# A graph layer on one core: single instead of double turns, gates per unit, and lists read after the stores of h

## The chip, the core and the metric

The kernel runs on one core of one Trainium2 chip. A core has five engines with a queue of their own each: TensorE (PE in the profile; its weight loads are shown apart as PEld), VectorE (DVE), ScalarE (ACT), GpSimd (POOL) and SyncE (SP, which here only issues transfers). Transfers are issued by SP, ScalarE or GpSimd and are done by 16 DMA engines. An engine works through its queue in order; an instruction that waits holds up all that is queued behind it. The metric is the device time of one launch in microseconds (us).

## The reference

The input is a graph with 6250 nodes of 256 features and 206250 edges that are sorted by target node, each with a polarity and 64 features. Cut to what matters:

```
h = max(layernorm(x), 0)                                  # every node
e = relu(raw @ W_e1.T + b_e1) @ W_e2.T + b_e2             # every edge, 64 -> 256 -> 256
edge_emb = (e * (clip(attr[:, 0], 0, 1) + 0.01)) @ W_le.T + b_le
msg  = relu(h[src] + edge_emb)                            # one row of h is gathered per edge
aggr = segment_sum(msg, dst)                              # 6250 rows
y = (h + aggr) @ W_g1.T + b_g1
out = x + relu(layernorm(y) * ln_g + ln_b) @ W_g2.T + b_g2
```

## The kernel before, in words

**Tiles.** Edges are taken in tiles of 128. Four tiles are a *block* (512 edges), two tiles a *unit* (256 edges), so a block has two units; two blocks are a *pair* (four units). There are 403 blocks, NU = 806 units and NP = 202 pairs. Six blocks are a *group*; the sums of a group are built up in PSUM.

**Start phase.** x is loaded in 13 parts of up to four times 128 rows. For each part VectorE takes the statistics, ScalarE applies layernorm and ReLU, GpSimd adds b_le (`hb`, four adds of 128x256 for a whole part, L470) and SP stores the part to `hb_d` in device memory. W_e2 and W_le are multiplied into one matrix `wc_s` in this phase. The edge parts of the first LEAD = 22 units are made here too. ScalarE's queue issues the reads of three lists of 806 KB: the source nodes `src_s`, the target nodes `dst_f` and the polarities `pol_s`; GpSimd casts `dst_f` to float at the end. The first four units gather rows of x itself, by a small list `src_0` of 8 columns. All other units gather rows of h from `hb_d`, so the first of these gathers stands behind the last store of h and behind the list `src_s`.

**What is done for a unit.** TensorE makes the edge part, 2 x 2 matmuls with `wc_s` into one PSUM bank (L347; a float32 matmul stands in the profile as two records, so a unit has 8). VectorE adds an offset and moves it to SBUF as `msg` (L353). GpSimd issues two gathers for the unit, one for each tile (L663), into one of HG = 20 places `hx`/`hg`. When a gather has landed, VectorE multiplies `msg` by the polarity and adds it to the gathered rows (the unit's two *products*, L718), and ScalarE applies ReLU to both halves (L725). Later TensorE sums the rows by target node with a 0/1 matrix `sel` (L740).

**What is done for a pair.** The first layer of the edge network, raw @ W_e1 (L310), runs for a whole pair, two pairs ahead: two halves of 128 features for each of two blocks, 4 matmuls (8 records) into 4 banks, two of them side by side in the two halves of the array's rows. ScalarE evicts three of the banks and VectorE one. The bias, ReLU and eviction are one instruction. Raw edge features for two pairs come in one transfer of 512 KB.

**PSUM.** Edge parts, first layers and node work take their banks from one ring of BANKS = 7. A matmul into a bank waits for the reader that emptied it seven takes earlier.

**The order of the work** is written out by the program. `forward(u)` emits the edge part of unit u, and behind unit u with u % 4 == TURN = 1 the *turn* (`turn_of`): first layers, sums and loads of raw. In the middle of the run (pairs FEW = 6 to NP - FEW - 1 = 195, `by_two`) a turn is done for two pairs at once, behind every eighth unit: sums of two pairs, then first layers of two pairs. Before and behind that it is done for each pair: first layer, then sums. A unit's products are due a number of units behind its edge part (`lag`), 18 at first and one less every SHRINK = 44 units, so TensorE starts 22 units ahead of the gathers and ends one unit ahead of them. Node work (layernorm, two 256x256 matmuls and two transposes for each of 49 windows of 128 nodes: L174, L189, L207, L220) is put between units in pieces, except directly around a turn (QUIET).

**When gathers are issued** is set by a planner. `in_step` (called as `paced`) adds up the planned TensorE time in `spent`: EDGE = 1.754 for a unit, LAYER = 0.9 for half a first layer, SUMS = 0.46 for the sums of a block, NODES = 0.81 for a node piece. A gather is planned at STEP = 1.288 each. At a *gate* (two places in a double turn's round: behind unit u % 8 == 5, and at the first layers) it emits all gathers up to `spent + AFLOAT + HALF`, where AFLOAT = 6.0 and HALF is half a round, 10.5; the first of them waits for the TensorE instruction at hand, the others for nothing but their places and lists.

**Lists and row numbers.** `first_rows` on TensorE reads `dst_f` (L566), and `rows_of_edges` on VectorE makes the row numbers from which `sel` is built.

Of the kernel before, what the change touches and what calls it, by code (L numbers as in the profile page):

```python
# [9 lines left out]
F32 = mybir.dt.float32  # L10
# [7 lines left out]
P = 128  # L18
N = 6250
D = 256  # L20
# [25 lines left out]
HALF = 4 * EDGE + 2 * LAYER + 2 * SUMS + NODES  # L46
BANKS = 7
SHRINK = 44
RAW = 4
HG = 16 + RAW  # L50
# [51 lines left out]
def gnn_kernel(ctx: ExitStack, tc: tile.TileContext, x, src_c, dst_c, dst_r, pol_c, raw_t, w_e1t, w_e2,  # L102
# [141 lines left out]
    with fast:  # L244
# [5 lines left out]
        msg_p = big.enter_context(tc.tile_pool(name="msg", bufs=LEAD + 2))  # L250
# [6 lines left out]
        evictions = {}  # L257
        places = [hx_p.tile([P, 2, D], F32, name=f"hx{i}") for i in range(RAW)]
        users = {}

# [23 lines left out]
        def load_pair(q):  # L284
            if q >= NP:
                return
# [9 lines left out]
        def first_layer(q):  # L296
# [7 lines left out]
            for c in range(2):  # L304
# [15 lines left out]
                paced(LAYER, z[c], c == 0 and not (by_two(q - 2) and q % 2))  # L320
# [17 lines left out]
        def edge_part(u):  # L338
# [10 lines left out]
            msg[u] = msg_p.tile([P, 2, D], F32, name="msg")  # L349
# [12 lines left out]
        paced = lambda us, behind, gate=False: None  # L362
# [40 lines left out]
        src_0 = const.tile([P, 2 * RAW], I32, name="src_0")  # L403
# [3 lines left out]
        nc.scalar.dma_start(out=src_0, in_=src_c[:, :2 * RAW])  # L407
# [25 lines left out]
        with tc.tile_pool(name="p1", bufs=4) as p1, tc.tile_pool(name="p1x", bufs=11) as p1x:  # L433
# [24 lines left out]
            def nodes_out(k):  # L458
# [10 lines left out]
                for i in range(t):  # L469
                    nc.gpsimd.tensor_add(hb[:p, i, :], xt[:p, i, :], ble_b[:p])  # L470
# [25 lines left out]
            rows_b = const.tile([P, 3, D], F32, name="rows_b")  # L496
            nc.scalar.dma_start(out=rows_b, in_=row_v.rearrange("(o r) d -> o r d", o=1).to_broadcast([P, 3, D]))
            ble_b, bg1_b, bg2_b = (rows_b[:, i, :] for i in range(3))
            load_rows(1)
            load_rows(2)  # L500
            load_rows(3)
            load_pair(2)
            load_rows(4)
            load_rows(5)
            load_pair(3)
# [3 lines left out]
            lists = {3: (src_s, src_c), 9: (dst_f.bitcast(I32), dst_c), 11: (pol_s, pol_c)}  # L509
# [703 lines left out]
```

## Time and profile before

| | us |
|---|---|
| median of 3 runs (2152.94 to 2156.09) | 2155.08 |
| the profiled execution | 2150.16 |
| its span, from the first to the last instruction | 2148.4 |
| TensorE busy | 2104.8 |
| VectorE busy | 1594.2 |
| ScalarE busy | 1010.0 |
| GpSimd busy | 1621.4 |

Rows of the timeline read: start, time, engine, line and operation, output<-input, partitions x elements, count, and in brackets the idle time ahead of the row with what ended it. A merged row's time runs to the end of its last instruction, which overlaps the first of the next row, so what a stretch costs is read from start to start. Rows of waits read: total us, times, longest. Groups read: count, busy us, mean ns of one, idle time ahead of them and what ended most of it. "issue" is idle time in which the engine waited for nothing that the profile shows.

### The profile page before, as it was taken

The page shows a single profiled execution, that of the slowest core. Times are in us where ns is not written, and L with a number is a line of the kernel's source. Part 1 is how long each engine was busy: PE and PEld are TensorE (multiplying, and loading weights), DVE is VectorE, ACT ScalarE, POOL GpSimd, SP SyncE. Part 2 cuts the span into 40 slices and gives each one's busy share as a digit, 9 for nine tenths or more (in the row PEclk, how much of TensorE's full clock was granted, in tenths as well). Part 3 has the DMA queues.
Part 4 walks back from the last instruction along what each step waited for, and adds up shares of the span by engine and source line. Part 5 has one row for each costly group of instructions (what it writes and reads, how often), then busy time and mean ns, then how long its engine had stood idle before and what let it go on. Part 6 is the DMA issues. An engine that isn't in the chain of part 4 may idle for free.

```text
span 2148.4 us, 33462 instructions
## 1 busy us (share of the span) xinstructions
PE 2104.8 (98%) x11940; PEld 1559.8 (73%) x11940; DVE 1594.2 (74%) x3455; ACT 1010.0 (47%) x1804; POOL 1621.4 (75%) x1675
## 2 busy tenths in 40 slices
PE   9999999999999999999999999999999999999998
PEld 6677776777777676777777776777777777777766
DVE  7888776877777777777777767776777777777776
ACT  7544444444444444444444444444544454444443
POOL 6777777777777777777777777777777777777775
PEclk9999999999999999999999999999999999999999
DMA  9544545455545444544454554455444455454543
GB/s 317 185 147 140 152 148 159 142 154 152 163 149 155 148 150 145 162 141 152 144 153 148 160 159 136 147 158 159 144 150 144 149 156 152 148 152 140 160 139 92
DMA packets 143638, 330.35 MB, mean 154 GB/s; under 512 B 35999, under 2 KB 71416, under 8 KB 142712
## 3 DMA queue, kind: packets, MB, share of 16 engines
q0 software_dynamic: 77376, 211.39, 34.2%
q1 hardware_dynamic: 64788, 113.47, 15.9%
q10 hardware_dynamic: 1300, 3.28, 0.4%
q8 instruction: 95, 1.56, 0.3%
q14 instruction: 79, 0.65, 0.1%
HBM read 306.24 MB, written 34.08 MB: 158 GB/s over the span
## 4 chain that ended last, share of the span: by engine, by line
PE 53%; POOL 26%; issue 11%; DMA 6%; DVE 3%; ACT 0%; SPq 0%; POOLq 0%; ACTq 0%; DVEq 0%
PE pz L347 35%; POOL hg L663 21%; PE pz L310 10%; POOL hx L663 5%; PE pd L740 4%; DMA hg<-hb_d,src_s 4%; PE pz L220 1%; DVE hg L718 1%; PE pz L189 1%; DMA raw<-in_raw_t_dram 1%; DVE msg L353 1%; DMA hx<-hb_d,src_s 1%; PE pz L207 0%; DVE st L159 0%; PE pz L174 0%
## 5 line engine op out<-in xcount | busy, mean ns | idle before, releaser
L663 POOL DMA_INDIRECT hg<-hb_d,src_s x1284 | 1259.7, 981 | 393.8 <-issue 368.6
L347 PE MATMUL pz<-wc_s,e 128*128 128x256 f32 x6448 | 1456.0, 382 | 2.1 <-DVE msg L353 2.1
L347 PEld LDWEIGHTS pz<-wc_s,e 128*128 128x128 f32 x6448 | 1212.0, 190 | 238.2 <-ACT e L327 74.1
L725 ACT ACTIVATE hg<-hg 128x512 f32<-128x512 f32 x641 | 404.2, 631 | 806.2 <-DVE hg L718 806.2
L718 DVE SCALAR_TENSOR_TENSOR hg<-msg,pol_s,hg 128x256 f32<-128x256 f32 x1284 | 591.4, 479 | 229.4 <-DMA hg<-hb_d,src_s 225.8
L353 DVE TENSOR_TENSOR msg<-pz,bc_s 128x512 f32<-128x512 f32 x799 | 542.3, 683 | 15.9 <-PE pz L347 15.2
L310 PE MATMUL pz<-raw,we_s 64*128 64x512 f32 x1612 | 384.0, 608 | 18.4 <-DVE msg L353 9.9
L663 POOL DMA_INDIRECT hx<-hb_d,src_s x320 | 316.8, 990 | 97.5 <-issue 92.9
L327 ACT ACTIVATE e<-pz,vecs 128x512 f32<-128x512 f32 x605 | 360.8, 693 | 60.3 <-PE pz L310 59.9
L324 DVE TENSOR_SCALAR e<-pz,vecs 128x512 f32<-128x512 f32 x201 | 150.6, 749 | 206.6 <-PE pz L310 206.2
L310 PEld LDWEIGHTS pz<-raw,we_s 64*128 64x128 f32 x1612 | 145.5, 187 | 211.1 <-issue 130.4
L725 ACT ACTIVATE hx<-hx 128x512 f32<-128x512 f32 x164 | 103.4, 631 | 195.1 <-DVE hx L718 195.1
L718 DVE SCALAR_TENSOR_TENSOR hx<-msg,pol_s,hx 128x256 f32<-128x256 f32 x328 | 151.8, 480 | 57.4 <-DMA hx<-hb_d,src_s 56.7
L740 PE MATMUL pd<-hg,sel 128*32 128x256 f32 x2560 | 160.4, 384 | 11.0 <-ACT hg L725 11.0
L740 PEld LDWEIGHTS pd<-hg,sel 128*32 128x32 f32 x2560 | 74.7, 110 | 82.0 <-issue 25.9
L694 DVE SCALAR_TENSOR_TENSOR sel<-iota_w,zero_c,rel 128x256 f32<-128x256 f32 x202 | 96.5, 478 | 0.0
L189 PE MATMUL pz<-wg_s,hT 128*128 128x256 f32 (+1 forms) x196 | 50.8, 382 | 0.8 <-ACT hT L178 0.8
L220 PE MATMUL pz<-wg_s,nT 128*128 128x256 f32 (+1 forms) x196 | 50.5, 380 | 0.9 <-ACT nT L211 0.9
L740 PE MATMUL pd<-hx,sel 128*32 128x256 f32 x656 | 43.5, 382 | 0.0
L189 PEld LDWEIGHTS pz<-wg_s,hT 128*128 128x128 f32 (+1 forms) x196 | 36.8, 190 | 7.6 <-ACT hT L178 1.2
L470 POOL TENSOR_TENSOR hb<-xt,rows_b 128x256 f32<-128x256 f32 (+1 forms) x49 | 34.1, 727 | 10.5 <-ACT e L327 3.5
L220 PEld LDWEIGHTS pz<-wg_s,nT 128*128 128x128 f32 (+1 forms) x196 | 37.0, 190 | 6.6 <-ACT nT L211 1.1
(113 smaller groups left out, 518.0 us busy)
## 6 DMA issues: line engine op xcount, KB each, us to landing
raw<-in_raw_t_dram SPq DMA_DIRECT2D x99, 512.0 KB
hg<-hb_d,src_s POOLq DMA_INDIRECT x1284
sum_d<-zero_d SPq DMA_DIRECT2D x47, 256.0 KB
ab<-sum_d SPq DMA_DIRECT2D x47, 256.0 KB
sum_d<-ms SPq DMA_DIRECT2D x264, 32.0 KB
hb_d<-hb SPq DMA_DIRECT2D x12, 512.0 KB
xt<-in_x_dram SPq DMA_DIRECT2D x48, 128.0 KB
out_dram<-ot SPq DMA_DIRECT2D x48, 128.0 KB
```

The source lines that it names most:

```text
L189: z = nc.tensor.matmul(ph[:n, 0, :], aT[:, c, :n], wg1_s[:, c, :], start=c == 0 and not bias_by_pe, stop=c == 1)
L220: z = nc.tensor.matmul(po[:n, 0, :], nT[:, c, :n], wg2_s[:, c, :], start=c == 0, stop=c == 1)
L310: z[c] = nc.tensor.matmul(pe[s, c], we1_s[s * F:(s + 1) * F, c * P:(c + 1) * P], raw[q][s * F:(s + 1) * F, :], start=True, stop=True)
L324: a = nc.vector.tensor_scalar(e1[b][:, c, :], pe[s, c], be1_s[:, c:c + 1], 0.0, op0=ALU.add, op1=ALU.max)
L327: a = nc.scalar.activation(e1[b][:, c, :], pe[s, c], AF.Relu, bias=be1_s[:, c:c + 1])
L347: last_z = nc.tensor.matmul(pz[:, i, :], e1[b][:, c, k:k + P], wc_s[:, c, :], start=c == 0, stop=c == 1)
L353: a = nc.vector.tensor_add(msg[u], pz, bc_s)
L663: g = nc.gpsimd.indirect_dma_start(out=hg[u][:, i, :], out_offset=None, in_=hb_d, in_offset=bass.IndirectOffsetOnAxis(ap=src_s[:, 2 * u + ...
L694: nc.vector.scalar_tensor_tensor(sel[g][:, k * S:k * S + n, :], iota_w.rearrange("p (o w) -> p o w", o=1).to_broadcast([P, n, W]), zero_c, ...
L718: product = nc.vector.scalar_tensor_tensor(hg[u][:, i, :], m[:, i, :], pol_s[:, 2 * u + i:2 * u + i + 1], hg[u][:, i, :], op0=ALU.mult, op ...
L725: done[u] = product, nc.scalar.activation(hg[u], hg[u], AF.Relu)
L740: z = nc.tensor.matmul(acc[g][j * W:(j + 1) * W, :], sel[g][:, k * S + j, :], m[:, j % 2, :], start=k == 0, stop=b == blocks_of(g)[-1])
```

## The change

It has six parts.

1. **Turns.** `turn_of` is the same for all pairs: behind every fourth unit the first layer of one pair, then the sums that are due, then, every second time, the loads.
2. **Sums later.** In the middle of the run, `add_pairs` takes only pairs whose last unit is at least LATER = 3 units behind the newest finished product.
3. **Products around the add.** `edge_part` calls `half_of_products` on both sides of the add of the new edge part: where a product is due, VectorE gets first half of the older unit, add, second half.
4. **Gates.** Each call of `paced` (behind each edge part and each half of a first layer) emits at most one unit's two gathers; the first waits for the TensorE instruction at hand. HALF is gone. Before the first call only the two gathers of unit 4 are emitted.
5. **Message buffers** are 24 named tiles used in turn instead of a pool of 24.
6. **Start.** The small lists `src_0` and `pol_0` have EARLY = 40 columns (20 units), and the gathers and products of the first 20 units use them. The full lists and two of the three bias rows are read by SP behind the stores of h; the cast of `dst_f` moves from GpSimd to VectorE, and it and the two passes over `pol_s` run behind unit 23 (`lists`), `first_rows` one unit later than that at the earliest. The adds of b_le of the last whole part are shared between GpSimd and VectorE. Loads of raw for pairs 2 and 3 are issued earlier, those for pairs 8 and 9 behind the stores.

```
-HALF = 4 * EDGE + 2 * LAYER + 2 * SUMS + NODES
+LATER = 3
+EARLY = 40
...
+        edges = [msg_p.tile([P, 2, D], F32, name=f"msg{i}") for i in range(LEAD + 2)]
...
-                paced(LAYER, z[c], c == 0 and not (by_two(q - 2) and q % 2))
+                paced(LAYER, z[c])
...
-            msg[u] = msg_p.tile([P, 2, D], F32, name="msg")
+            msg[u] = edges[u % (LEAD + 2)]
+            half_of_products(u, 0)
             if plain(u):
                 a = nc.scalar.activation(msg[u], pz, AF.Copy)
             else:
                 a = nc.vector.tensor_add(msg[u], pz, bc_s)
             ps.read(a)
-            apart_from(a, before)
+            apart_from(a, before, *users.get(u - LEAD - 2, ()))
+            half_of_products(u, 1)
...
-            paced(EDGE, last_z, by_two(u // 4) and u % 8 == 5)
+            paced(EDGE, last_z)
...
         def turn_of(q):
-            if not by_two(q):
-                if q + 2 < NP:
-                    first_layer(q + 2)
-                sums(q == NP - 1)
-                if q % 2 == 0:
-                    load_pair(q + 4)
-                    load_pair(q + 5)
-            elif q % 2 == 0:
-                sums(False)
+            if q + 2 < NP:
                 first_layer(q + 2)
-                first_layer(q + 3)
+            sums(q == NP - 1)
+            if q % 2 == 0:
                 load_pair(q + 4)
                 load_pair(q + 5)
...
-                    nc.gpsimd.tensor_add(hb[:p, i, :], xt[:p, i, :], ble_b[:p])
+                    eng = nc.vector if k == len(parts) - 2 and i % 2 else nc.gpsimd
+                    eng.tensor_add(hb[:p, i, :], xt[:p, i, :], ble_b[:p])
...
-                if k in lists:
-                    t, src = lists[k]
-                    nc.scalar.dma_start(out=t, in_=src[:, :NT])
-            nc.gpsimd.tensor_copy(dst_f, dst_f.bitcast(I32))
+            for q in postponed:
+                load_pair(q, True)
+            nc.sync.dma_start(out=src_s, in_=src_c[:, :NT])
+            nc.sync.dma_start(out=dst_f.bitcast(I32), in_=dst_c[:, :NT])
+            nc.sync.dma_start(out=pol_s, in_=pol_c[:, :NT])
...
-            def in_step(us, behind, gate=False):
+            def in_step(us, behind):
                 nonlocal spent
                 spent += us
-                while gate and (got - 2 * RAW) * STEP < spent + AFLOAT + HALF and got < 2 * min(NU, 4 * summed + HG):
+                if got % 2 == 0 and (got - 2 * RAW) * STEP < spent + AFLOAT and got < 2 * min(NU, 4 * summed + HG):
                     gather(behind)
-                    behind = None
+                    gather()
...
-                while summed + pairs < NP and min(4 * (summed + pairs) + 4, NU) < made + last:
+                while summed + pairs < NP and min(4 * (summed + pairs) + 4, NU) < made - eager + last - (0 if last or summed > NP - 2 * FEW else LATER):
...
+            def half_now(u, i):
+                nonlocal made, eager
+                if i == 0:
+                    eager = by_two(u // 4) and made < due_at(u)
+                    if eager:
+                        gathers(made + 1)
+                if eager:
+                    products(made, i)
+                    made += i
```

On TensorE, in the middle of the run, a turn stands as follows before the change (L740 sums, L310 first layer, L347 edge parts); of the sums only the last row is shown:

```order
L740 MATMUL pd<-hg_843,sel 32x256 x2
L310 MATMUL pz_118<-raw,we_s 128x512
L310 MATMUL pz_119<-raw,we_s 128x512
L310 MATMUL pz_120<-raw,we_s 128x512
L310 MATMUL pz_121<-raw,we_s 128x512
L310 MATMUL pz_122<-raw,we_s 128x512
L310 MATMUL pz_123<-raw,we_s 128x512
L310 MATMUL pz_124<-raw,we_s 128x512
L310 MATMUL pz_118<-raw,we_s 128x512
L347 MATMUL pz_119<-wc_s,e_111 128x256 x4
```

And with the change, at the same place (L766 are the sums, L316 the first layer, L353 the edge parts):

```order
L316 MATMUL pz_143<-raw,we_s 128x512
L316 MATMUL pz_144<-raw,we_s 128x512
L316 MATMUL pz_145<-raw,we_s 128x512
L316 MATMUL pz_146<-raw,we_s 128x512
L766 MATMUL pd<-hg_845,sel 32x256 x2
L766 MATMUL pd<-hg_846,sel 32x256 x2
L766 MATMUL pd<-hg_847,sel 32x256 x2
L766 MATMUL pd<-hg_848,sel 32x256 x2
L353 MATMUL pz_147<-wc_s,e_113 128x256 x4
```

Eight first-layer matmuls in a row, whose last takes the bank of the first again, have become four, and the sums of one pair stand behind them. TensorE has 107 stretches of first-layer matmuls before and 202 now, 101 and 196 of sums, and 296 and 391 of edge parts; the number of matmuls is the same.

On GpSimd, the end of the start phase and the first gathers of rows of h before the change, with what each waits for (Activation, DVE, PE are engines, DMAHW and DMASW transfers that have landed):

```order
L470 TENSOR_TENSOR hb<-xt,rows_b 106x256 [waits DMAHW4_49,DMAHW5_49,Activation_49,Pool_49]
L539 CAST dst_f<-dst_f 128x1612 [waits DMAHW4_49]
L663 DMA hg_832<-hb_d,src_s 128x256 [waits DMAHW2_49,DMAHW3_49,DMAHW1_49,DMAHW6_49,DMASW0_49,DMAHW7_49,DVE_49,Pool_49]
L663 DMA hg_832<-hb_d,src_s 128x256 [waits DMASW1_49]
L663 DMA hg_833<-hb_d,src_s 128x256 [waits DMASW2_49]
```

And with the change (L679 are the gathers):

```order
L473 TENSOR_TENSOR hb<-xt,ble_b 106x256 [waits DMAHW4_49,DMAHW5_49,Activation_49,Pool_49]
L679 DMA hg_837<-hb_d,src_172 128x256 [waits DMAHW1_49,DMAHW5_49,DMAHW0_49,DMAHW6_49,DMASW0_49,DMAHW7_49,DVE_49,Pool_49]
L679 DMA hg_837<-hb_d,src_172 128x256 [waits DMASW1_49]
L679 DMA hg_838<-hb_d,src_172 128x256 [waits DMASW2_49,PE_49]
L679 DMA hg_838<-hb_d,src_172 128x256 [waits DMASW3_49]
L679 DMA hg_839<-hb_d,src_172 128x256 [waits DMASW4_49,PE_49]
```

The cast is gone from GpSimd, and from the third gather on every second one waits for TensorE; before, the first of these waits came at the fourteenth gather.

On VectorE, in the middle of the run, before the change (L353 is the add of a new edge part, L718 the products of an older unit):

```order
L353 TENSOR_TENSOR msg<-pz_121,bc_s 128x512 [waits PE_49]
L718 SCALAR_TENSOR_TENSOR hg_836<-msg,pol_s,hg_836 128x256 [waits DMASW0_49,DVE_49]
L718 SCALAR_TENSOR_TENSOR hg_836<-msg,pol_s,hg_836 128x256 [waits DMASW1_49]
L353 TENSOR_TENSOR msg<-pz_122,bc_s 128x512 [waits PE_49]
L718 SCALAR_TENSOR_TENSOR hg_837<-msg,pol_s,hg_837 128x256 [waits DMASW2_49,DVE_49]
```

And with the change (L360 is the add, L728 the products):

```order
L728 SCALAR_TENSOR_TENSOR hg_840<-msg_133,pol_s,hg_840 128x256 [waits DMASW6_49]
L360 TENSOR_TENSOR msg_120<-pz_146,bc_s 128x512 [waits PE_49,Activation_49]
L728 SCALAR_TENSOR_TENSOR hg_840<-msg_133,pol_s,hg_840 128x256 [waits DMASW7_49]
L728 SCALAR_TENSOR_TENSOR hg_841<-msg_134,pol_s,hg_841 128x256 [waits DMASW0_49]
L360 TENSOR_TENSOR msg_121<-pz_147,bc_s 128x512 [waits PE_49]
L728 SCALAR_TENSOR_TENSOR hg_841<-msg_134,pol_s,hg_841 128x256 [waits DMASW1_49]
```

The add has moved between the two halves: it stands now behind the first half's wait for its gather and ahead of the second half's.

More of the change, by code (lines that the diff above doesn't have):

```diff
@@ L282, in gnn_kernel, with load_pair @@
         ps = Ring()
-        def load_pair(q):
+        def load_pair(q, now=False):
             if q >= NP:
+                return
+            if q in (8, 9) and not now:
+                postponed.append(q)
                 return
@@ L561, in node_weights, with lists @@
             nc.sync.dma_start(out=wg2_s, in_=vec(w_g2t))
+        def lists():
+            nc.vector.tensor_copy(dst_f, dst_f.bitcast(I32))
+            nc.vector.tensor_scalar(pol_s, pol_s, 0.0, 1.0, op0=ALU.max, op1=ALU.min)
+            nc.vector.tensor_scalar_add(pol_s, pol_s, 0.01)
         def first_rows():
@@ L714, in whole @@
                     nc.vector.tensor_add(m, m, bc_s)
[L715 to L727 removed]
+            def whole(u, between=lambda: None):
+                products(u, 0)
+                between()
+                products(u, 1)
             def add_up(b, newest=()):
@@ L945, in due @@
                 fns = todo.pop(now, deque())
-                if fns and not (by_two(now // 4) and now % 8 in QUIET):
+                if fns and not (by_two(now // 4) and now % 4 in QUIET):
                     spent += NODES
```

86 lines of the change are left out of this document (47 added, 39 removed).

## The prediction

> **What bounds the kernel now.** I read the page's head and its list of engines first.
>
> ```profile
> PE 2104.8 (98%) x11940; PEld 1559.8 (73%) x11940; DVE 1594.2 (74%) x3455; ACT 1010.0 (47%) x1804; POOL 1621.4 (75%) x1675
> PE 53%; POOL 26%; issue 11%; DMA 6%; DVE 3%; ACT 0%; SPq 0%; POOLq 0%; ACTq 0%; DVEq 0%
> ```
>
> TensorE looks full at 98%, but the second line, the chain that ended last, gives POOL and "issue" 37% together, so a second chain runs through the gathers. The timeline of POOL shows it: its end of the start phase, and its last gather.
>
> ```profile
> 57.17 3.46 POOL L470 TENSOR_TENSOR hb<-xt,rows_b 128x256 f32<-128x256 f32 x5 [0.17 <-POOL hb L470]
> 60.59 1.52 POOL L539 CAST dst_f<-dst_f 128x1612 f32<-128x1612 int32 x1
> 64.99 0.98 POOL L663 DMA_INDIRECT hg<-hb_d,src_s  x1 [2.88 <-DVE st L159]
> ...
> 67.52 0.95 POOL L663 DMA_INDIRECT hg<-hb_d,src_s  x1 [0.30 <-issue]
> ...
> 2128.96 0.94 POOL L663 DMA_INDIRECT hg<-hb_d,src_s  x1 [0.30 <-issue]
> ...
> L663 POOL DMA_INDIRECT hg<-hb_d,src_s x1284 | 1259.7, 981 | 393.8 <-issue 368.6
> L663 POOL DMA_INDIRECT hx<-hb_d,src_s x320 | 316.8, 990 | 97.5 <-issue 92.9
> ```
>
> 1284 + 320 = 1604 gathers lie between 64.99 and 2129.90, 1.2874 us each, and the idle time ahead of them is nearly all the 0.30 us of issue. POOL issues back to back for the whole run: 65.0 + 2064.9, and 18.5 us of tail after the last one make the span. TensorE has some room beside it. Its busy time and instructions in the stretch of the gathers (second and third column; the fifth pair is POOL's):
>
> ```profile
> 66.00:2128.00 2062.00, 2031.64 (x11588) 1506.90 (x11588) 1537.25 (x3266) 959.68 (x1700) 1573.97 (x1602) 1.00 0.50 150
> core 0: 2148.4 us, clock 0.996
> ```
>
> 30.4 us of idle, and a granted clock of 0.996, which costs 0.4% of 2063 us or 8.3 us. What ends TensorE's waits and VectorE's:
>
> ```profile
> DVE hg L718 <- DMA hg<-hb_d,src_s: 225.8, 290, 3.6
> DVE hx L718 <- DMA hx<-hb_d,src_s: 56.7, 71, 2.6
> PE pd L740 <- ACT hg L725: 11.0, 7, 2.7
> PE pz L310 <- DVE msg L353: 9.9, 13, 1.4
> ```
>
> VectorE waits 361 times for a gather. TensorE's own waits are behind that: sums whose rows have come late, and first-layer products without a free bank.
>
> **The turns, which is the main term.** One double turn as it is now (sums of two pairs, first layer of two pairs, then eight units of products L347), and one single turn, which this kernel runs near its end:
>
> ```profile
> 917.62 1.93 PE L740 MATMUL pd<-hg,sel 128*32 128x256 f32 x32
> 919.48 3.70 PE L310 MATMUL pz<-raw,we_s 64*128 64x512 f32 x16
> 923.12 1.99 PE L347 MATMUL pz<-wc_s,e 128*128 128x256 f32 x8
> 924.95 0.38 PE L174 MATMUL pz<-ident,stb 128*128 128x128 f32 x2
> 925.17 5.35 PE L347 MATMUL pz<-wc_s,e 128*128 128x256 f32 x24
> 930.35 1.03 PE L189 MATMUL pz<-wg_s,hT 128*128 128x256 f32 x4
> 931.21 7.07 PE L347 MATMUL pz<-wc_s,e 128*128 128x256 f32 x32
> 938.21 1.93 PE L740 MATMUL pd<-hg,sel 128*32 128x256 f32 x32
> ```
> ```profile
> 2097.03 1.99 PE L310 MATMUL pz<-raw,we_s 64*128 64x512 f32 x8
> 2098.95 1.07 PE L740 MATMUL pd<-hg,sel 128*32 128x256 f32 x16
> 2099.95 1.99 PE L347 MATMUL pz<-wc_s,e 128*128 128x256 f32 x8
> 2101.78 0.38 PE L174 MATMUL pz<-ident,stb 128*128 128x128 f32 x2
> 2102.00 1.89 PE L347 MATMUL pz<-wc_s,e 128*128 128x256 f32 x8
> 2103.73 0.38 PE L207 MATMUL pz<-ident,hs 128*128 128x128 f32 x2
> 2103.95 3.62 PE L347 MATMUL pz<-wc_s,e 128*128 128x256 f32 x16
> 2107.50 1.98 PE L310 MATMUL pz<-raw,we_s 64*128 64x512 f32 x4
> ```
>
> I take distances from start to start. Double: 938.21 - 917.62 = 20.59, less the node pieces inside (L174 0.22, L189 0.86) = 19.51 us for eight units. Single: 2107.50 - 2097.03 = 10.47, less L174 and L207 (0.22 each) = 10.03 us for four. Two singles cost 20.06: 0.55 us more for the same matmuls. The parts show where: 1.92 us for 8 first-layer records against 3.64 for 16, 1.00 for 16 sum records against 1.86 for 32, so 0.20 and 0.14 us, and the remaining 0.21 is at the edges of L347. Each is a change of the matmul's shape (128*128, 64*128, 128*32), and single turns make twice as many. By the bounds FEW and NP - FEW, pairs 6 to 195 run doubled now: 95 double turns, so the change adds 95 x 0.55 = 52 us to TensorE. No instruction is taken away for it.
>
> The Trainium skill speaks against this part too: "TensorEngine Tiling (Array Packing)", Key Properties, says that changing the tiling mode drains the engine, and the rows above agree. With the 128 cycles at 2.4 GHz that "TensorE: Matmul & The Clock Gate" (Step-by-step) gives for a drain, an estimate is 53 ns a change, 3 x 95 x 0.053 = 15 us in place of 52; the rows have the switch itself, so the measurement is used.
>
> What hides these 52 us? From the first-layer product behind unit 21 to the end of the last unit's product there are 784 units:
>
> ```profile
> 64.90 1.99 PE L310 MATMUL pz<-raw,we_s 64*128 64x512 f32 x8
> 66.81 1.99 PE L347 MATMUL pz<-wc_s,e 128*128 128x256 f32 x8
> ...
> 78.26 1.13 PE L310 MATMUL pz<-raw,we_s 64*128 64x512 f32 x4 [1.39 <-DVE msg L353]
> 81.41 1.13 PE L310 MATMUL pz<-raw,we_s 64*128 64x512 f32 x4 [2.02 <-ACT e L327]
> ...
> 2127.57 1.07 PE L740 MATMUL pd<-hg,sel 128*32 128x256 f32 x16
> ```
>
> 2127.57 - 64.90 = 2062.7 us, of the span of 2148.4. Without any stall this takes now 95 x 19.51 + 6 x 10.03 + 47 x 2.16 (node pieces of a window: 0.86 twice, 0.22 twice; I take L220 like L189) = 2015 us. So 47.6 us are slack: 30.4 idle, 8.3 clock, 9 stretched inside busy records. With single turns throughout it takes 196 x 10.03 + 101.5 = 2067.4, which is 4.7 us more than now with no stall at all. The clock's 8.3 us come on top. The cover is used up: TensorE becomes the bound, and the gathers, whose chain was late, get company.
>
> **How much stall stays.** Nothing to all of it: 0 to 39 us (47.6 - 8.3). Three rows say it is near the lower end. A double turn needs eight banks of a ring of seven, so its last first-layer product waits for an eviction of the same turn (78.26 and 81.41 above, 3.4 us in one place); a single turn needs four. The sums move three units behind the newest product (LATER), which is some 7.5 us (three times 10.03/4), above the longest 2.7 us of the wait for ReLU. And gathers are issued every 2.575 us a unit, against (2067.4 + 8.3)/784 = 2.648 us a unit on TensorE. Against zero stands the new order on VectorE: the add of unit u stands behind the first product of an older unit, so a late gather now holds that add, and who waits for the add is TensorE, for its bank. The bank comes round some 6 us later (two units, first layer, sums), while the longest wait for a gather was 3.6 us, so it mostly does not reach TensorE. I take 8 us.
>
> **Gates per unit.** Each pair of gathers now waits for one TensorE instruction, released 6.0 us ahead of the planner's clock. Two issues take 2.57 us, and a slow gather took this long to land (the chain, in order of time):
>
> ```profile
> 1158.31 5.57 DMA hg<-hb_d,src_s
> ```
>
> 2.57 + 5.57 is more than 6.0, so POOL can no longer run far ahead after TensorE has stalled. Behind a waiting gather only gathers are queued. This is in the 8 us; its bound above is in the 39.
>
> **The start.** The first gather stands behind the last store of h. POOL loses two of 49 adds (1.4 us by the row at 57.17, 0.69 each) and the cast of 1.52 us, and the three lists of 806 KB no longer load beside the stores. Gather 8 can start 1.4 us earlier, and at most 5.8 if the store then took nothing (the adds end at 60.63 now, 1.4 sooner 59.2). But gathers 10 and 11 wait for unit 22's product, which ends at about 68.6 (66.81 and eight records), while gather 10 was issued at 67.5 in the run of now: the lead is lost at the gate. For TensorE the gain is a wait for raw, when the lists no longer load beside it:
>
> ```profile
> 37.83 1.99 PE L310 MATMUL pz<-raw,we_s 64*128 64x512 f32 x8 [1.59 <-DMA raw<-in_raw_t_dram]
> ```
>
> On the other side, the cast (bounded by POOL's 1.52 us above) and the two passes over pol_s, which VectorE has now too, stand on VectorE behind unit 23's add and wait for lists that SP issues after the stores.
>
> ```profile
> 0.00:66.00 66.00, 61.12 (x272) 44.97 (x274) 48.97 (x168) 46.05 (x94) 45.83 (x72) 1.00 0.91 304
> ```
>
> 3.2 MB (raw, lists, a row) at the 304 GB/s of the start's row take 10.5 us, so they land about 73; the cast's reader on TensorE comes behind unit 26, about 77.5. Cost 0 to 3 us, and add 24 is queued behind it. Gain and cost: -2 to +5, I take -1. The first product on a gathered unit now holds back the add of unit 26; before, that add stood behind an earlier half. The named message buffers change no instruction, and a buffer's last reader is two units older than its writer: 0. The tail has the same order on TensorE: 0.
>
> **Sum.** 4.7 + 8.3 + 8 - 1 = +20 us. The profiled execution took 2150.16 us for its span of 2148.4; the median of the runs, 2155.08, is 4.9 us above it. I add the 20 to the median: 2175 us.
>
> **Rivals.** (a) The stalls stay as they are: gates and the add behind a product keep both chains in lockstep. For it: 361 waits on VectorE; against it: the bank rule above. 4.7 + 8.3 + 39 - 1 = +51, 2206 us. (b) Within 0.2%: the gathers' chain still sets the end, because a change of shape costs less in mid-run than at the end. The extra 0.55 us would have to be 0.41 or less (2015 + 8.3 + 95 x 0.41 is the 2062.7 of now). Time 2155 us. Against it: both distances come from this trace without a wait in them. By the Trainium skill's drain alone (the 15 us estimated above) it would come out so. (c) Faster: the earlier first gather moves the whole chain of 1604 by its 1.4 to 5.8 us, at most to 2149 us; for it is that POOL is back to back now. It decides from 4.3 us on, and only where unit 22's gate opens before 64 and TensorE has slack as in (b).
>
> **Chances.** Forecast (up to 35 us slower) 0.70, (a) 0.16, (b) 0.09, (c) 0.05. A change under 0.2% (4.3 us) can't be told from none here. Slower 0.86, same 0.09, faster 0.05. The range leaves out (c) and the far end of (a): 2157 to 2202; the forecast's own is 2160 to 2190.
>
> **What would show it.** Right: TensorE's first-layer groups of 8 records, 1.92 us apart from the sums; busy TensorE near 2150; gathers with waits for TensorE of more than 0.3 us in their idle time; no wait of a sum for ReLU. Wrong: gathers still back to back with 18.5 us behind the last; single turns under 9.9 us; waits of the first layer for the adds that grow, which would be (a).

## The result and the profile after

The changed kernel takes 2167.18 us (median of 5 runs, 2166.46 to 2169.7), the kernel before 2155.08 in the runs beside it. The ratio is 1.006, with a 95% interval of 1.0048 to 1.0072: 0.6% slower. The profiled execution took 2168.57 us for a span of 2166.9.

The page after the change: busy time of the engines, the chain that ended last by engine, and the two large groups of gathers.

```profile
PE 2145.4 (99%) x11940; PEld 1534.6 (71%) x11940; DVE 1609.8 (74%) x3460; ACT 992.1 (46%) x1804; POOL 1630.1 (75%) x1672
PE 92%; DVE 2%; DMA 1%; issue 1%; POOL 0%; ACT 0%; SPq 0%; DVEq 0%; ACTq 0%; POOLq 0%
...
L679 POOL DMA_INDIRECT hg<-hb_d,src_s x1252 | 1231.9, 984 | 381.5 <-issue 323.9
...
L679 POOL DMA_INDIRECT hx<-hb_d,src_s x320 | 317.6, 992 | 97.5 <-issue 81.3
```

The busy share moved by a point, from 98% to 99%; the chain tells the change. It was 53% TensorE with 37% POOL and issue, and is 92% TensorE now. The gathers are still issued back to back, with 0.30 us of idle ahead of nearly each, but they no longer set the end: from the start of the last one to the end of the span it takes 26.4 us (2166.9 - 2140.48), against 19.4 before. The stretches of the profile show when TensorE became the bound (second and third column: TensorE's busy time and instructions):

```profile
66.00:200.00 134.00, 125.41 (x673) 87.73 (x672) 113.42 (x228) 58.59 (x106) 103.23 (x97) 0.99 0.51 160
200.00:2100.00 1900.00, 1899.92 (x10663) 1360.58 (x10662) 1404.54 (x2966) 863.43 (x1559) 1451.16 (x1474) 1.00 0.50 150
```

From 200 to 2100 us TensorE is idle for 0.08 us. Nearly all of its idle time in the gathers' stretch, 8.6 us, lies in the first 200 us. The waits (total, times, longest) turned round with it:

```profile
DVE msg L360 <- PE pz L353: 288.0, 475, 1.4
...
DVE hg L728 <- DMA hg<-hb_d,src_s: 51.3, 68, 3.5
...
POOL hg L679 <- PE pz L353: 27.4, 82, 2.7
```

VectorE waited 225.8 us for gathers before; now it waits 51.3 us for them and 288 us for TensorE. The gates hardly hold POOL: 82 of the gathers into `hg` are released by an edge part, at 0.3 us each but for one of 2.7.

### The profile page after: what moved, and what is told of

It is laid out like the page before. It is cut to its first block, busy times and chain, and to the rows that moved or that the text cites. A ratio compares the mean times of both kernels' runs of the same rounds, so it can differ in the third digit from the quotient of the medians.

```text
span 2166.9 us, 34025 instructions
## 1 busy us (share of the span) xinstructions
PE 2145.4 (99%) x11940; PEld 1534.6 (71%) x11940; DVE 1609.8 (74%) x3460; ACT 992.1 (46%) x1804; POOL 1630.1 (75%) x1672
## 4 chain that ended last, share of the span: by engine, by line
PE 92%; DVE 2%; DMA 1%; issue 1%; POOL 0%; ACT 0%; SPq 0%; DVEq 0%; ACTq 0%; POOLq 0%
PE pz L353 62%; PE pz L316 17%; PE pd L766 9%; PE pz L190 2%; PE pz L221 2%; DMA hg<-hb_d,src_s 1%; DVE hg L728 1%; PE pz L208 0%; PE pz L175 0%; DVE msg L360 0%; POOL hg L679 0%; DMA stb<-st_d 0%; DMA sum_d<-ms 0%; DVE sel L710 0%; DVE hx L728 0%
## 5 line engine op out<-in xcount | busy, mean ns | idle before, releaser
L679 POOL DMA_INDIRECT hg<-hb_d,src_s x1252 | 1231.9, 984 | 381.5 <-issue 323.9
L353 PE MATMUL pz<-wc_s,e 128*128 128x256 f32 x6448 | 1479.4, 383 | 6.3 <-DVE msg L360 6.3
L353 PEld LDWEIGHTS pz<-wc_s,e 128*128 128x128 f32 x6448 | 1201.8, 190 | 244.1 <-DVE e L330 44.5
L360 DVE TENSOR_TENSOR msg<-pz,bc_s 128x512 f32<-128x512 f32 x799 | 550.1, 689 | 295.2 <-PE pz L353 288.0
L728 DVE SCALAR_TENSOR_TENSOR hg<-msg,pol_s,hg 128x256 f32<-128x256 f32 x1252 | 574.8, 478 | 52.7 <-DMA hg<-hb_d,src_s 51.3
L316 PE MATMUL pz<-raw,we_s 64*128 64x512 f32 x1612 | 402.1, 615 | 1.5 <-DVE msg L360 1.2
L679 POOL DMA_INDIRECT hx<-hb_d,src_s x320 | 317.6, 992 | 97.5 <-issue 81.3
L333 ACT ACTIVATE e<-pz,vecs 128x512 f32<-128x512 f32 x605 | 368.7, 679 | 9.7 <-PE pz L316 9.6
L316 PEld LDWEIGHTS pz<-raw,we_s 64*128 64x128 f32 x1612 | 138.8, 186 | 164.5 <-issue 146.8
L766 PE MATMUL pd<-hg,sel 128*32 128x256 f32 x2560 | 171.0, 385 | 0.0
L766 PEld LDWEIGHTS pd<-hg,sel 128*32 128x32 f32 x2560 | 67.3, 109 | 145.0 <-issue 86.3
L728 DVE SCALAR_TENSOR_TENSOR hx<-msg,pol_s,hx 128x256 f32<-128x256 f32 x320 | 148.2, 479 | 11.2 <-DMA hx<-hb_d,src_s 11.1
L221 PE MATMUL pz<-wg_s,nT 128*128 128x256 f32 (+1 forms) x196 | 51.3, 385 | 0.9 <-ACT nT L212 0.9
L679 POOL DMA_INDIRECT hg<-hb_d,src x32 | 38.5, 1204 | 14.8 <-issue 8.2
L766 PE MATMUL pd<-hx,sel 128*32 128x256 f32 x656 | 43.9, 385 | 1.7 <-ACT hx L735 1.7
L766 PEld LDWEIGHTS pd<-hx,sel 128*32 128x32 f32 x656 | 17.1, 109 | 39.6 <-issue 23.5
```

The costliest lines, as they stand in the source:

```text
L221: z = nc.tensor.matmul(po[:n, 0, :], nT[:, c, :n], wg2_s[:, c, :], start=c == 0, stop=c == 1)
L316: z[c] = nc.tensor.matmul(pe[s, c], we1_s[s * F:(s + 1) * F, c * P:(c + 1) * P], raw[q][s * F:(s + 1) * F, :], start=True, stop=True)
L333: a = nc.scalar.activation(e1[b][:, c, :], pe[s, c], AF.Relu, bias=be1_s[:, c:c + 1])
L353: last_z = nc.tensor.matmul(pz[:, i, :], e1[b][:, c, k:k + P], wc_s[:, c, :], start=c == 0, stop=c == 1)
L360: a = nc.vector.tensor_add(msg[u], pz, bc_s)
L679: g = nc.gpsimd.indirect_dma_start(out=hg[u][:, i, :], out_offset=None, in_=hb_d, in_offset=bass.IndirectOffsetOnAxis(ap=of_tile(src_0, sr ...
```

## The experiments

Each group of kernels ran on one chip beside the kernel before. The first group had the kernel before at 2151.73 us (25 runs), the pair a_noeager_2 and d_noeager_2 had it at 2152.55 (17 runs). On two further chips TensorE was granted less, and the kernel before took 2519.12 and 2516.59 us; those two groups stand at the end and are read by themselves. The changed kernel itself was in another group, with the kernel before at 2155.08, so kernels of different groups are compared by their ratios.

The theory (turns): single turns add some 0.55 us of TensorE for every pair of them, 95 times, which uses up TensorE's slack. The rival (gates): the gathers now wait for TensorE, and the whole chain of gathers comes late. LATER, the named message buffers and the order of the node work were not run by themselves.

**Double turns back in the middle (a_double81).** From the changed kernel, 81 double turns:

```diff
+        def in_twos(q):
+            return 20 <= q < NP - 20
...
-            if q + 2 < NP:
-                first_layer(q + 2)
-            sums(q == NP - 1)
-            if q % 2 == 0:
+            if not in_twos(q):
+                if q + 2 < NP:
+                    first_layer(q + 2)
+                sums(q == NP - 1)
...
+            elif q % 2 == 0:
+                sums(False)
+                first_layer(q + 2)
+                first_layer(q + 3)
```

> The changed kernel with double turns (sums of two pairs, then first layers of two pairs) for pairs 20 to 181, 81 double turns; gates, products around the add, LATER and the start as changed. Turn theory (single turns cost TensorE 0.55 us a pair of turns, and TensorE is the bound): TensorE loses 81 x 0.55 = 45 us of work, the chain of gathers takes over, which ended at 2141.4 us in the changed kernel; the time falls by 4 to 16 us to 2151 to 2163 us, TensorE shows 25 us or more of idle time. Gate theory (the gathers' chain, held at its gates, is what became longer, by the 11.5 us by which the last gather starts later): the gates are the same, so 2164 to 2169 us.

Measured: 2158.51 us (2155.42 to 2160.68), ratio 1.0029 (1.0017 to 1.0041). The time is in the range of the turn theory and below that of the gates. By the ratios, 1.0029 against 1.006, 81 x 0.55 = 45 us of work taken from TensorE bring back some 6.7 us of time. Where the rest went stands in the stretches of this kernel, the chain that ended last, and TensorE's longest wait:

```profile
66.00:1000.00 934.00, 914.22 (x5171) 674.79 (x5170) 698.97 (x1484) 432.32 (x767) 713.36 (x721) 0.99 0.50 151
1000.00:2130.00 1130.00, 1116.44 (x6379) 825.89 (x6378) 828.99 (x1772) 522.65 (x926) 862.81 (x878) 1.00 0.50 150
...
PE 78%; DMA 5%; DVE 4%; POOL 4%; issue 4%; ACT 1%; ACTq 0%; POOLq 0%; DVEq 0%
...
PE pz L316 <- ACT e L333: 21.5, 18, 2.1
```

TensorE is idle again for 19.8 and 13.6 us, so it is no longer the only bound. Behind 200 us it waits for free banks: first-layer matmuls wait 21.5 us for ScalarE's evictions, ahead of the last banks that a double turn takes. The sums wait 0.2 us for a ReLU, where the kernel before had 11.0 us of that.

The gathers' chain is late too. Its last gather starts at 2134.67 us against 2128.96 before the change, but POOL and issue hold only 8% of the chain that ended last, against 37% before. Of these 5.7 us of lateness, 4.3 are there at the 33rd gather (113.3 against 109.0 us): the first 32 gathers take 38.8 us on POOL, 34.3 before. The changed kernel has 38.5 there, a_nogate 38.9 and a_noeager_2 38.5, but b_start 35.6, so neither the wait at the gates nor the adds between the products make it alone; which part of the change does is open.

**Single turns alone (b_single).** From the kernel before, with the same gates as before at every second pair:

```diff
-            if not by_two(q):
-                if q + 2 < NP:
-                    first_layer(q + 2)
-                sums(q == NP - 1)
-                if q % 2 == 0:
+            if q + 2 < NP:
+                first_layer(q + 2)
+            sums(q == NP - 1)
+            if q % 2 == 0:
...
-            elif q % 2 == 0:
-                sums(False)
...
-                lag = max(LEAST, LEAD - RAW - u // SHRINK) + (by_two(u // 4) and (u + 1) % 8 == TURN)
+                lag = max(LEAST, LEAD - RAW - u // SHRINK) + (by_two(u // 4) and (u + 1) % 4 == TURN)
...
-                if fns and not (by_two(now // 4) and now % 8 in QUIET):
+                if fns and not (by_two(now // 4) and now % 4 in QUIET):
```

> The kernel before with single turns and nothing else of the change (node pieces kept off units u % 4 of 0 and 1 instead of u % 8, the lag's extra unit likewise). Turn theory: 196 x 10.03 + 101.5 = 2067 us of work without stall behind unit 21 against 2062.7 taken before, plus 6 us of clock and up to 8 of stall: 10 to 19 us slower, 2165 to 2174 us. Gate theory: the gates are those of before, so no change, 2152 to 2158 us.

Measured: 2160.9 us (2159.72 to 2162.39), ratio 1.0041 (1.0027 to 1.0055), 9.2 us over the kernel before. Its profile says the same as that of the changed kernel:

```profile
core 0: 2158.0 us, clock 0.999
...
1000.00:2130.00 1130.00, 1130.00 (x6335) 809.92 (x6332) 834.44 (x1771) 532.22 (x926) 848.38 (x877) 1.00 0.50 149
...
PE pz L347 <- DVE msg L353: 2.3, 2, 1.7
...
PE pz L575 <- DVE msg L353: 1.1, 1, 1.1
...
PE pz L310 <- DVE msg L353: 0.4, 1, 0.4
```

From 1000 to 2130 us TensorE is never idle, and the single turns alone make it the bound. The time is under the range I expected of the theory, because two of its terms were smaller: the waits for adds are 3.8 us in place of up to 8, and from the first layer behind unit 21 (64.25 us) to the last sums on `hg` (2137.14) it takes 2072.9 us, which leaves 1.7 us beside the 2067.4 without a stall and these waits, in place of the 6 for the clock. With the 4.7 us of longer turns and a start that is 0.65 us earlier that is 9.6 us, as the two profiled executions lie apart (2158.0 - 2148.4); the medians lie 9.2 apart. The span of the changed kernel is 8.9 us longer than this one: 4.8 of it are more waits for adds, 2.9 the tail.

**No gates (a_nogate).** From the changed kernel; no gather waits for TensorE:

```diff
-                    gather(behind)
+                    gather()
                     gather()
```

> The changed kernel in which the gathers are emitted at the same places but do not wait for TensorE (they wait for their places and lists as before). Turn theory: TensorE stays the bound; only the 5 us of idle time between 133 and 170 us, where adds wait behind late gathers, can shrink: 2162 to 2167 us. Gate theory: the chain of gathers gets its 11.5 us back: 2154 to 2158 us.

Measured: 2165.15 us (2164.35 to 2165.78), ratio 1.0056 (1.0039 to 1.0073). That is in the range of the turn theory, and the rival's 2154 to 2158 is out. Its profile has the 100th gather 2.1 us earlier than the changed kernel (198.24 against 200.32), and TensorE busy for all of 1000 to 2130 us again.

**The new start alone (b_start).** From the kernel before: lists behind the stores, two of the adds of h on VectorE, 40 early indices; turns, gates, adds and message buffers as before:

```diff
-        src_0 = const.tile([P, 2 * RAW], I32, name="src_0")
+        src_0 = const.tile([P, EARLY], I32, name="src_0")
+        pol_0 = const.tile([P, EARLY], F32, name="pol_0")
...
-                    nc.gpsimd.tensor_add(hb[:p, i, :], xt[:p, i, :], ble_b[:p])
+                    eng = nc.vector if k == len(parts) - 2 and i % 2 else nc.gpsimd
+                    eng.tensor_add(hb[:p, i, :], xt[:p, i, :], ble_b[:p])
...
+            nc.sync.dma_start(out=src_s, in_=src_c[:, :NT])
```

> The kernel before with the new start alone (lists read by SP behind the stores of h, short lists for the first 20 units, cast and passes on VectorE behind unit 23, shared adds), with its double turns, its gates, its order of products. Turn theory: the chain of gathers is the bound there and starts 2.4 us earlier (62.57 against 64.99): 2151 to 2154 us. If the early start were lost to the lists on VectorE or to longer gathers beside the lists: 2155 to 2160 us.

Measured: 2153.23 us (2147.88 to 2159.23), ratio 1.0004 (0.9992 to 1.0016): no difference that can be told. The one profiled execution, the fastest of its 12 runs, has the whole chain of gathers ahead by the 2.4 us of its first one, and a span of 2146.2 in place of 2148.4:

```profile
62.54 0.96 POOL L686 DMA_INDIRECT hg<-hb_d,src  x1 [2.88 <-DVE st L161]
...
2126.57 0.95 POOL L686 DMA_INDIRECT hg<-hb_d,src_s  x1 [0.30 <-issue]
```

Runs of the kernel before spread over 12 us, so 2.2 us of one execution are not a result.

**Adds ahead of the products again, with single turns and with double ones (a_noeager_2, d_noeager_2).** What was expected refers to the first runs of both, which are told below. Beside the adds, the edit puts the node work back to its old place: the change calls a step of it (`piece`) ahead of the products, before it stood behind the first of them. From the changed kernel, and for the second from a_double81 with message buffers from a pool as before the change:

```diff
-            half_of_products = half_now
...
-                piece()
+                between = piece
                 while made < due_at(u):
                     gathers(made + 1)
-                    whole(made, piece)
+                    whole(made, between)
                     made += 1
+                    between = lambda: None
+                if between is piece:
+                    piece()
```

> The kernel of a_noeager again (single turns, gates per unit, new start; each unit's add of message parts ahead of the products), because there both it and the kernel before ran at 2470 to 2540 us with a granted clock of 0.955 to 0.97, so that it can't be set beside the 2155 and 2167 us. If the kernel before runs near 2152 us here: turn theory 2161 to 2165 us (only the stalls between 130 and 170 us go); rival, the adds come late without the change: over 2168 us with TensorE idle between 200 and 2100 us. If the clock is again below 0.97, a ratio near 0.983, as there.

> The kernel of d_noeager again (the changed kernel with double turns for pairs 20 to 181, message buffers from a pool, no adds between products), for the same reason. If the kernel before runs near 2152 us: 2153 to 2156 us if the adds between products are what kept double turns at 2158.5 us, 2157 to 2160 us if it is the gates per unit or the stalls of the first 200 us. If the clock is again below 0.97, a ratio near 0.996.

Measured with single turns: 2164.42 us (2163.78 to 2166.44), ratio 1.0055 (1.0043 to 1.0067), within the range expected. The reason I gave carries only a part of it. Between 130 and 170 us TensorE waits 2.89 us for adds in place of 5.04. The larger part in this profile is the tail, which goes with the place of the node work (see the tail below): from the start of the last sums of L766 on `hg` to the end it takes 20.9 us (2141.16 to 2162.1), against 23.7 in the changed kernel. By the ratios alone, 1.0055 and 1.006, the two can't be told apart.

Measured with double turns: 2154.05 us (2151.7 to 2158.04), ratio 1.0005 (0.9996 to 1.0013). By the ratios that is some 5 us under a_double81, whose interval (1.0017 to 1.0041) doesn't meet this one, so with double turns the adds between products, the new place of the node work and the named message buffers cost about that together; this edit takes all three back at once, and how they cost it is not shown. The gathers' mean is 988 ns against 987 in a_double81, so the sign I had named, 984 ns or less, did not come. TensorE's waits behind 200 us are as long, 23.8 us against 24.0, but are for other things:

```profile
PE pz L315 <- DVE msg L359: 22.3, 17, 3.0
```

In a_double81 the first layers wait for ScalarE's evictions, here for VectorE's adds. But the profiled execution of this kernel is its slowest run (2158.04), 4 us over its median, so its trace can't show what was saved. On the same chip, single against double turns without these adds are 2164.42 against 2154.05, 10.4 us for the turns (and the pool of message buffers).

**Chips that grant TensorE less (a_noeager, d_noeager, d_nogate, s_raw6).** d_nogate is a_double81 with the edit of a_nogate. s_raw6 was meant to beat both kernels: b_start with more units gathered from x ahead of the stores of h, so that the chain behind the stores is shorter.

```diff
-RAW = 4
+RAW = 6
...
-HG = 16 + RAW
+HG = 20
...
-AHEAD = 10
+AHEAD = 9
...
-tc.tile_pool(name="p1x", bufs=11)
+tc.tile_pool(name="p1x", bufs=10)
```

> The changed kernel without the edge parts added between an older unit's products: each unit's add of message parts comes ahead of the products again, as before; single turns, gates per unit and the new start stay. Turn theory: TensorE stays the bound from 200 us on, so only the stalls between 130 and 170 us can go, where the add stood behind products that waited for late gathers (about 5 us of TensorE idle): 2161 to 2165 us. Rival, the order of the adds is what made single turns bearable (VectorE's add comes late without it and TensorE waits for a bank in the middle): over 2168 us, with TensorE idle between 200 and 2100 us.

> The changed kernel with double turns for pairs 20 to 181, and in addition without the adds between products (message buffers from a pool, as before). Double turns alone gave 2158.5 us, 3 to 5 us above the kernels with all of the old order, with TensorE idle again and the gathers' chain 4 to 5.7 us behind. If the adds between products hold VectorE and with it the gathers' buffers or lengthen the gathers: 2153 to 2156 us, the gathers' mean at or below 984 ns. If the gates per unit make the rest: 2157 to 2160 us, the 100th gather still at 200 us or later.

> The changed kernel with double turns for pairs 20 to 181, and in addition no gather waits for TensorE. If the gates make the rest of the 3 to 5 us: 2153 to 2156 us, the 100th gather near 198 us. If the adds between products do: 2157 to 2160 us. If it is the stalls of the first 200 us, which both leave: both kernels stay at 2157 to 2160 us.

> The kernel before with the new start alone, and six units instead of four gathered from x ahead of the stores of h (reads of x nine parts ahead instead of ten; 20 gather buffers as before). If the chain of gathers is what bounds a kernel with double turns, four gathers fewer behind the stores take 4 x 1.284 = 5.1 us off it: 2147 to 2150 us. If the start pays for it (four more pairs of statistics on VectorE, 80 to 85% busy there) or TensorE is the bound at once: 2152 to 2156 us.

The times neither meet nor refute these expectations, since the kernel before took 2519.12 us there. The ratios: a_noeager 0.9828 (0.9791 to 0.9865, 2476.53 us), d_noeager 0.9964 (0.9938 to 0.9989), s_raw6 0.9957 (0.9932 to 0.9983), d_nogate 1.2279 (1.222 to 1.2338, 3095.84 us). What TensorE does in d_nogate there:

```profile
1011.83 1.89 PE L353 MATMUL pz<-wc_s,e 128*128 128x256 f32 x8
...
1019.70 0.58 PE L353 MATMUL pz<-wc_s,e 128*128 128x256 f32 x1 [0.82 <-issue]
1021.10 0.59 PE L353 MATMUL pz<-wc_s,e 128*128 128x256 f32 x1 [0.81 <-issue]
```

Eight matmuls of a product take 1.89 us, and then single ones start 1.40 us apart, with nothing that the profile shows to wait for. Two kernels ran again, s_raw6 and d_nogate, and came to a second chip of this kind:

> The kernel of s_raw6 again (the kernel before with the new start alone, six units instead of four gathered from x ahead of the stores of h, reads of x nine parts ahead, 20 gather buffers). If the kernel before runs near 2152 us: 2147 to 2150 us if the chain of gathers bounds the kernel with double turns (4 x 1.284 = 5.1 us less of it behind the stores); 2152 to 2156 us if the start pays for it (more statistics on VectorE, fewer reads ahead) or TensorE is the bound at once. If the clock is below 0.97, a ratio near 0.996, as there.

> The kernel of d_nogate again (the changed kernel with double turns for pairs 20 to 181, no gather waits for TensorE). If the kernel before runs near 2152 us: since the adds between products alone took double turns from 2158.5 to 2154 us, the gates should be worth 0 to 2 us: 2156 to 2159 us. Rival, the ratio of 1.228 on the chip whose TensorE was held back belongs to the kernel (gathers with no wait run ahead until they wait for the sums, and TensorE is granted less): above 2200 us here too.

Measured: s_raw6_2 2509.18 us, ratio 0.9957 (0.9933 to 0.998); d_nogate_2 3099.63 us, ratio 1.2297 (1.2245 to 1.235), against 2516.59. Both repeat, on another chip. Whether six early units pay where TensorE is not held back stays open, and so does what d_nogate would take there. On the chips with a full clock no version was measured under the kernel before.

## Why the prediction was right, and where it was off

**The turns** were the main term, and hold. A single turn in the middle of the changed kernel:

```profile
1012.42 1.99 PE L316 MATMUL pz<-raw,we_s 64*128 64x512 f32 x8
1014.34 1.07 PE L766 MATMUL pd<-hg,sel 128*32 128x256 f32 x16
1015.34 7.17 PE L353 MATMUL pz<-wc_s,e 128*128 128x256 f32 x32
1022.44 1.99 PE L316 MATMUL pz<-raw,we_s 64*128 64x512 f32 x8
```

1022.44 - 1012.42 = 10.02 us with no node piece in it, against the 10.03 read from the end of the kernel before. So a pair of turns costs 2 x 10.02 - 19.51 = 0.53 us more, not the 0.41 or less that rival (b) needed. Busy TensorE is 2145.4 us, where I had named 2150. The drain priced by the Trainium skill ("TensorE: Matmul & The Clock Gate", Step-by-step; an estimate of 15 us for all changes of shape) would have left TensorE in the cover. This trace doesn't bear that out: 95 x 0.53 is 50 us.

**The stalls** were put at 8 us, and are 8.6. That the two lie so close is luck: I had given them no place, and as causes late gathers that hold an add, and the gates. They all lie in the first 200 us, and only 5.0 us have one of these causes:

```profile
77.35 0.71 PE L578 MATMUL pz<-dst_f,ones 1*128 1x268 f32 x2 [1.09 <-DVE msg L360]
79.46 7.13 PE L353 MATMUL pz<-wc_s,e 128*128 128x256 f32 x24 [1.28 <-DVE msg L360]
99.08 1.13 PE L316 MATMUL pz<-raw,we_s 64*128 64x512 f32 x4 [1.18 <-DVE msg L360]
...
166.75 1.99 PE L353 MATMUL pz<-wc_s,e 128*128 128x256 f32 x8 [2.47 <-DVE msg L360]
```

The first two, 2.4 us, stand behind the cast and the two passes over the lists on VectorE, which the prediction had at 0 to 3 us in its term for the start, not here:

```profile
72.64 0.99 DVE L571 CAST dst_f<-dst_f 128x1612 f32<-128x1612 int32 x1
73.55 0.99 DVE L572 TENSOR_SCALAR pol_s<-pol_s 128x1612 f32<-128x1612 f32 x1
74.58 1.00 DVE L573 TENSOR_SCALAR pol_s<-pol_s 128x1612 f32<-128x1612 f32 x1
```

The third, 1.2 us, is an add behind the making of the row numbers on VectorE (L602 to L604, 96.45 to 98.15 us). The other six, 5.0 us between 133 and 170, are the adds behind the products of late gathers, as forecast; a_noeager_2, without that order, has 2.9 there. After 200 us VectorE still waits for a gather now and then, but no such wait reaches TensorE. Rival (a), lockstep at 39 us, is out: of VectorE's 361 waits for gathers some 90 are left, since TensorE is the slower of the two.

**The start** gained 1.6 us on TensorE (its L316 behind unit 21 starts at 63.33 in place of 64.90), of which b_single has 0.65 with the old start. With the 2.4 us of stalls behind the lists the start costs 0.8 us, where the forecast had -1. The gathers gained nothing, as forecast: the lead is lost at the gate.

```profile
62.57 0.96 POOL L679 DMA_INDIRECT hg<-hb_d,src  x1 [2.94 <-DVE mv L161]
63.83 0.95 POOL L679 DMA_INDIRECT hg<-hb_d,src  x1 [0.30 <-issue]
67.51 0.94 POOL L679 DMA_INDIRECT hg<-hb_d,src  x1 [2.74 <-PE pz L353]
...
2140.48 0.95 POOL L679 DMA_INDIRECT hg<-hb_d,src_s  x1 [0.30 <-issue]
```

The third gather starts at 67.51 us, as it did at 67.52 before. This one wait was all: the sign "gathers with waits for TensorE of more than 0.3 us" was wrong as a sign for the run.

**The tail** was put at 0, by "the same order on TensorE", and is 2.9 us: 2166.9 - 2143.17 = 23.7 from these sums on `hg`, against 20.8 before. That step overlooked VectorE. The sums that follow wait for a ReLU, the ReLU for a product, and the product stands behind a step of node work that waits for a read of `st_d`:

```profile
2141.95 0.35 DVE L914 SCALAR_TENSOR_TENSOR hT<-hT,zero_c,stb 128x128 f32<-128x128 f32 x1 [1.44 <-DMA stb<-st_d]
2142.22 0.48 DVE L728 SCALAR_TENSOR_TENSOR hx<-msg,pol_s,hx 128x256 f32<-128x256 f32 x1
...
2143.17 1.07 PE L766 MATMUL pd<-hg,sel 128*32 128x256 f32 x16
2145.99 1.07 PE L766 MATMUL pd<-hx,sel 128*32 128x256 f32 x16 [1.75 <-ACT hx L735]
```

Before the change the product stands ahead of that step:

```profile
2124.83 0.48 DVE L718 SCALAR_TENSOR_TENSOR hx<-msg,pol_s,hx 128x256 f32<-128x256 f32 x1
2125.22 0.34 DVE L888 SCALAR_TENSOR_TENSOR hT<-hT,zero_c,stb 128x128 f32<-128x128 f32 x1
```

It is the change's new place of the node work, which its six parts don't name, and a read issued late behind stores of sums. With the old place, a_noeager_2 has no wait at these sums; which of the two weighs more is open. It is not the gathers: VectorE waits for none of them behind 2130 us. Their chain is longer, 990 ns a gather in the mean over all 1604 against 983 before, so that the last one starts 11.5 us later (4.2 us of this in the first 32), but TensorE does not wait for that.

**The clock** was put at 8.3 us, from the mean of 0.996 over the whole span. What is left of the middle, 2143.17 - 63.33 = 2079.8 less 2067.4 without a stall less 8.6 of waits, is 3.8. The stretches above have a granted clock of 0.99 up to 200 us and 1.00 from there, so no row shows 8.3 us; that the 3.8 are the clock is not shown either.

**The sum**: 4.7 + 3.8 + 8.6 - 1.6 + 2.9 = 18.4 us, where the forecast had 4.7 + 8.3 + 8 - 1 = 20: the clock too high and the tail too low, which cancel for the most part. Against the profiled execution of before that gave 2170 and it was 2168.57. Beside these two terms, the step that was off is the last one, adding the 20 to the median of 2155.08: the medians lie only 12.1 us apart. The profiled execution of before stood 4.9 us under its own median, that of after 1.4 above its own. In the other two groups the kernel before has medians of 2151.73 and 2152.55 us, so a part of the 4.9 belongs to the few runs here. The kernel before spreads (2147.48 to 2159.45 over 25 runs), the kernels with single turns less (2166.46 to 2169.7 over 5 runs of the changed kernel, 2159.72 to 2162.39 over 8 of b_single); why is not shown. Of a kernel whose profiled execution lies low among its runs, the median has less to lose than the profile. 2167.18 is inside the range, 8 us under the point.

## What to carry to other kernels

An engine at 98% in a kernel whose chain runs through another engine has slack that can be counted: the length of its pattern without stalls, times the number of patterns, against the time between its first and last instruction. A reordering that adds work per pattern is free only up to that count; here 52 us were put on 47.6 us of slack, and the time grew by the difference, with start-up stalls, a tail and a remainder on top, not by the 52. A step put ahead of others in one engine's queue brings its own waits with it, as the tail shows. And add a forecast made against one execution to that execution, and ask separately where it lies among the runs: here the spread of the runs changed with the bound.

## What the runs showed of the hardware that was not expected

The mean time of one indirect gather of 128 rows on POOL is not a constant: over all 1604 it is 975 ns in b_single, 981 in a_noeager_2, 983 before, and 990 in the changed kernel, with the same data. The ends differ by 15 ns, or 25 us of the chain. Most gathers take 0.95 us, and the spread comes from those over 1.0 us: 209 in b_single with 1.15 us in the mean, 370 before with 1.10, 355 in the changed kernel with 1.14. What makes them long is not shown.

Two of the chips held TensorE back in this one-core program: the granted clock was 0.94 to 0.97, where the runs elsewhere had 0.992 to 0.999, with single matmuls 1.40 us apart in one kernel. The clock in the records is not the whole of it: the same kernel has TensorE busy for 2282.8 us in a_noeager and 2144.1 in a_noeager_2, and idle for 198 and 18 us, while VectorE's busy time did not grow (1576.2 and 1604.4). How much was held back hung on the kernel. The kernel with single turns (a_noeager) had a clock of 0.969 there and a ratio of 0.983 to the kernel before, double turns 0.956 (d_noeager, 0.996), and double turns with adds between the products and no gates 0.87 (1.228, on both chips). So the order that is slower by 0.55% with a full clock is faster by 1.7% with a held clock. What in the order of instructions decides this is open: no run here takes it apart.
